# Layer norm, attention and a ternary feed-forward on one core: keys and queries by Strassen's seven products

## The chip, the cores and the metric

The kernel runs on one core of a Trainium2 chip. The core has a matrix engine (TensorE, PE in the profile; its weight loads are shown apart as PEld), a vector engine (VectorE, DVE), an engine for functions of one argument (ScalarE, ACT), a general engine (GpSimd, POOL) and an engine that mainly issues DMAs (SyncE, SP). ACT and POOL can issue DMAs too. Each engine works through its own queue in order; across engines they wait for each other by semaphores. Data sits in SBUF (128 partitions); TensorE writes to PSUM[...].

The metric is the device time of one execution in microseconds, as the median of several runs. A profiled execution, a run of its own, gives the trace.

## The reference

The input x has 2048 tokens of 256 values. With xn the layer norm of x, the result is x + attention(xn) + ffn(xn). Attention has 16 heads of 128 values; the feed-forward has ternary weights and a hidden width of 704.

```python
qkv = jnp.einsum('bsd,ed->bse', x, Wqkv)          # 3 x 16 heads x 128
q, k, v = ...
logits = jnp.einsum('bqhd,bkhd->bhqk', q, k) * D ** (-0.5)
w = softmax(logits)
out = jnp.einsum('bhqk,bkhd->bqhd', w, v).reshape(B, S, H * D)
return jnp.einsum('bse,de->bsd', out, Wout)
...
hidden = jax.nn.sigmoid(x1) * x2                   # x1, x2: xn by quantized w1, w2
return _bitlinear(hidden, w3)
```

Per head, q and k are each a product of a 128 x 256 weight with the 256 x 2048 transposed xn.

## The kernel before

All matmuls of the attention are in fp32. The transposed xn (`xnT`, 128 x 2 x 2048: the 256 features as two chunks of 128 partitions) stays in SBUF. The 2048 tokens are four blocks of 512 (`QB`), each of four tiles of 128 queries. The work of the attention is a list of 64 `blocks`, 16 heads by 4 token blocks, hence 256 tiles `v`.

The feed-forward is done first, up to about 103 us; it leaves its part of the result, with x added, in the four tiles `ys` in SBUF, one per token block. The attention's output adds to them head after head, and the last head's sums are stored from there.

One loop (L544) runs over the tiles. The order of every engine's queue is the order of the program's text (`tc.manual_schedule`). In an iteration tile `v` gets its scores, and tile `u = v - 6` (`LEAD`) is weighted; `n, t` are block and tile of `u`, and `h, b` head and token block of `v`. In a tile:

- `scores` (L421): four matmuls of 128 x 512, two into each of two PSUM tiles "s" of two banks (three such tiles exist); after each half VectorE takes the maximum (`mx`, L439), then the negated maximum of both (`nm`, L444), and ScalarE the two exps (L452), whose results are the halves `p`.
- `exchanged` (L458): 16 DMAs of 64 KB that move 32-partition groups of `p` into `part` (three buffers), the first ten issued by SP, the other six by ACT.
- `transposed` (L473): VectorE transposes 32 x 32 blocks of `part` of tile `v - 2` into `pT`, in two instructions of 1024 elements.
- `weighted` (L481): four of the block's sixteen matmuls with v into the bank "av"; the block's last is followed by a copy to `oT` by ScalarE.
- by `t`, one further piece of work, all through a single PSUM bank "m" (pool `ps_m`): t = 0 a piece of v for a later group of two heads (`v_piece`, L126), t = 1 the output of the block before, in two halves (`projected`, L505, with sums into `ys` at L521 by VectorE), t = 2 a piece of k of the next head (`k_piece`, L100, copied to `kT` by ScalarE, L110), t = 3 a piece of q (`q_piece`, L112, scaled and copied at L121).

Because `v - u` is 6, t = 2 and t = 3 are the first and second tile of a block in the counting of `v`. A piece of k or q is two matmuls of 128 x 512 that accumulate over the two feature chunks. Keys are stored in an order of columns that suits the exchange: k's matmul reads `xnT` in runs of 32 columns (`xnT_k`, L98).

The weights wq and wk of two heads (a group `G`) come in by one DMA each on SP (`load_weights`, L73), as do those of v and of the output.

Of the kernel before, what the change touches and what calls it, by code (L numbers as in the profile page):

```python
# [8 lines left out]
F32 = mybir.dt.float32  # L9
F32R = mybir.dt.float32r  # L10
AF = mybir.ActivationFunctionType
ALU = mybir.AluOpType
# [7 lines left out]
def layernorm_attention_bitffn_kernel(  # L20
# [14 lines left out]
    nc = tc.nc  # L35
    P = 128
    S, DM = x.shape
    FF = w1T.shape[1]
    D = P
    HD = woutT.shape[0]  # L40
    H = HD // D
    KC = DM // P
    QB = 512
    NB = S // QB
    TB = QB // P
    NKT = S // P
    KQ = NKT // TB
    HALF = S // 2
    FC = -(-FF // P)
    G = 2  # L50
# [13 lines left out]
    make_identity(nc, ident)  # L64


    ys = [const.tile([P, TB, DM], F32, tag=f"y{c}", name=f"y{c}") for c in range(NB)]
    xnT = const.tile([P, KC, S], F32, tag="xnT", name="xnT")

    weights = {}  # L70
    lead_in = True

    def load_weights(g: int, what: str):  # L73

        if what == "o":
            w = wpool.tile([P, G, DM], F32, tag="wo", name=f"wo{g}", bufs=2)
            src = woutT[g * G * D : (g + 1) * G * D, :].rearrange("(h p) e -> p h e", p=P)
        else:
            w = wpool.tile([P, KC, G * D], F32, tag=f"w{what}", name=f"w{what}{g}")
            lo = "qkv".index(what) * HD + g * G * D  # L80
            src = wqkvT[:, lo : lo + G * D].rearrange("(c p) e -> p c e", p=P)
        nc.sync.dma_start(w, src)
        weights[g, what] = w


# [26 lines left out]
    def q_piece(h: int, c: int):  # L112
        w = weights[h // G, "q"]
        pm = bank([P, QB], f"pq{h}_{c}")
        for d in range(KC):
            nc.tensor.matmul(  # L116
                pm, w[:, d, bass.ts(h % G, D)], xnT[:, d, bass.ts(c, QB)],
                start=(d == 0), stop=(d == KC - 1),
            )
        qT = kvpool.tile([P, QB], F32, tag="qT", name=f"qT{h}_{c}", bufs=NB + 1)  # L120
        nc.scalar.activation(qT, pm, AF.Copy, scale=SCALE)  # L121
        qTs[h, c] = qT

    NV = NKT // 2

# [15 lines left out]
    ppool = ctx.enter_context(tc.tile_pool(name="ppool", bufs=2))  # L141
    front = ExitStack()
    fw = front.enter_context(tc.tile_pool(name="ffw", bufs=1))


    def loads(fraw):
# [186 lines left out]
    def added(c: int):  # L333

        yT = yTs.pop(c)
        if c < NB - 1:
            pt = ps_s.tile([P, 2, QB], F32, tag="s", name=f"pyt{c}")
            pts = [pt.rearrange("p a (b e) -> p (a b) e", e=DM)]
        else:
            pts = [bank([P, 2, DM], f"pyt{c}_{u}") for u in range(2)]  # L340
        m = TB // len(pts)
        for u, pt in enumerate(pts):
            for t in range(m):
                for e in range(DM // P):
                    nc.tensor.transpose(  # L345
                        pt[:, t, bass.ts(e, P)], yT[:, e, bass.ts(u * m + t, P)], ident
                    )
            y = ys[c][:, u * m : (u + 1) * m]
            nc.vector.tensor_tensor(y, pt, y, ALU.add)


    with tc.manual_schedule():
# [63 lines left out]
    SP_DMAS = 10  # L416

    blocks = [(h, b) for h in range(H) for b in range(NB)]
    sums, rinvs, oTs, parts, pTs, avs = {}, {}, {}, {}, {}, {}

    def scores(v: int, amid=None, late=None):  # L421

        n, t = divmod(v, TB)
        h, b = blocks[n]
        halves, ps = [], []
        mx = small.tile([P, 2], F32, tag="mx", name=f"mx{v}")  # L430
        for i in range(2):
            s = ps_s.tile([P, HALF], F32, tag="s", name=f"s{v}_{i}")
            for j in range(HALF // QB):
                nc.tensor.matmul(  # L434
                    s[:, bass.ts(j, QB)], qTs[h, b][:, bass.ts(t, P)],
                    kTs[h][:, i * HALF + j * QB : i * HALF + (j + 1) * QB],
                    start=True, stop=True,
                )
            nc.vector.tensor_reduce(mx[:, i : i + 1], s, AX.X, ALU.max)  # L439
            halves.append(s)  # L440
            if i == 0 and amid:
                amid()
        nm = small.tile([P, 1], F32, tag="nm", name=f"nm{v}")
        nc.vector.tensor_reduce(nm, mx, AX.X, ALU.max, negate=True)  # L444
        if t == 0:
            sums[n] = small.tile([P, TB, 2], F32, tag="sum", name=f"sum{n}")
        if late:
            late()
        part = ppool.tile([P, NQ, S // NQ], F32, tag="part", name=f"part{v}", bufs=3)
        for i, s in enumerate(halves):  # L450
            p = ppool.tile([P, HALF], F32, tag="p", name=f"p{v}_{i}", bufs=4)
            nc.scalar.activation(  # L452
                p, s, AF.Exp, bias=nm, accum_out=sums[n][:, t, i : i + 1],
            )
            ps.append(p)
        parts[v] = ps, part

    def exchanged(v: int):  # L458
        ps, part = parts[v]
        for j in range(NQ):  # L460
            for g in range(NQ):
                (nc.scalar if NQ * j + g >= SP_DMAS else nc.sync).dma_start(
                    part[bass.ts(j, 32), g, :],
                    ps[j // 2][bass.ts(g, 32), bass.ts(j % 2, S // NQ)],
                )

    def inverses(n: int):
        ri = small.tile([P, TB], F32, tag="ri", name=f"ri{n}")
# [4 lines left out]
    def transposed(v: int):  # L473
        n, t = divmod(v, TB)
        if t == 0:
            pTs[n] = apool.tile([P, TB, NQ, S // NQ], F32, tag="pT", name=f"pT{n}")
        part = parts.pop(v)[1]
        for g in range(0, NQ, 2):
            nc.vector.transpose(pTs[n][:, t, g : g + 2], part[:, g : g + 2])  # L479

    def weighted(n: int, k: int, part=None):  # L481

# [22 lines left out]
    def projected(n: int, u: int, pool=ps_m, tag: str = "m"):  # L505

        h, b = blocks[n]

        m = 1 if n == NBK - 1 and u else 2
        pms = []  # L510
        for j in range(2):
            if j % m == 0:
                pm = pool.tile([P, m, DM], F32, tag=tag, name=f"po{n}_{u}_{j}")
            pms.append(pm[:, j % m, :])
            nc.tensor.matmul(  # L515
                pms[j], oTs[n, 2 * u + j], weights[h // G, "o"][:, h % G, :],
                start=True, stop=True,
            )
        for j in range(2):
            t = 2 * u + j  # L520
            nc.vector.scalar_tensor_tensor(  # L521
                ys[b][:, t, :], pms[j], rinvs[n][:, t : t + 1], ys[b][:, t, :],
                ALU.mult, ALU.add,
            )

            if h == H - 1 and (j or n == NBK - 1):
                t0 = t if n == NBK - 1 else t - 1
                (nc.scalar if n == NBK - 1 and j else nc.sync).dma_start(
                    out[b * QB + t0 * P : b * QB + (t + 1) * P, :].rearrange(
                        "(t p) d -> p t d", p=P  # L530
                    ),
                    ys[b][:, t0 : t + 1, :],
                )

    NBK = len(blocks)
    GB = G * NB
# [6 lines left out]
    with tc.manual_schedule():  # L543
        for u in range(-LEAD, (NBK - 1) * TB):  # L544
            n, t = divmod(u, TB)
            v = u + LEAD
            lead_in = u < 0
            if v < NBK * TB:

                scores(  # L550
                    v,
                    amid=(lambda: added(NB - 1)) if v == 1 else None,
                    late=(lambda: [summed(fp, c, f) for c, f in chunks[-2:]]) if v == 0 else None,
                )
                h, b = blocks[v // TB]

            if lead_in:
                for what, hg, i in first.get(v, ()):
                    {"q": q_piece, "k": k_piece, "v": v_piece}[what](hg, i)
                if v == 1:  # L560
                    front.close()
                    apool = ctx.enter_context(tc.tile_pool(name="apool", bufs=2))
                    load_weights(1, "v")
            elif t == 0:
                g = n // GB + 1
                if g < H // G and ("v", g, n % GB) not in made:
# [7 lines left out]
            elif t == 2:  # L574
                if n % GB == 1 and n // GB + 1 < H // G:
                    load_weights(n // GB + 1, "o")
            if v < NBK * TB and h + 1 < H:
                if v % TB == 0 and ("k", h + 1, b) not in made:
                    k_piece(h + 1, b)
                elif v % TB == 1 and ("q", h + 1, b) not in made:  # L580
                    q_piece(h + 1, b)
                if h % G == 0 and b == NB - 1 and h // G + 1 < H // G:
                    if v % TB == 2:
                        load_weights(h // G + 1, "k")
                    elif v % TB == 3:
                        load_weights(h // G + 1, "q")
            if v < NBK * TB and t != TB - 1:
                exchanged(v)
            if u >= 0:
                for k in range(t * KQ, (t + 1) * KQ):  # L590
                    weighted(n, k)
            if v < NBK * TB and t == TB - 1:
                exchanged(v)
            if u == (NBK - 1) * TB - 1:
                inverses(NBK - 2)
                inverses(NBK - 1)
            if v > 1 and v - 2 < NBK * TB:
                transposed(v - 2)
            if u >= 0 and t == 1 and n:
                projected(n - 1, 1)  # L600

        n = NBK - 1
        for k in range(NKT):
# [46 lines left out]
```

## Time and profile before

| what | value |
|---|---|
| median of 3 runs | 2285.8 us (2285.75 to 2285.82) |
| the profiled execution | 2285.53 us, its span 2283.7 us |
| VectorE: maxima of the scores, L439 | 512 instructions of 1224 ns mean |
| VectorE: transposes, L479 | 512 of 1222 ns |
| VectorE: sums into y, L521 | 256 of 478 ns |
| ScalarE: exp, L452 | 512 of 1109 ns |
| ScalarE: copies of k (L110), q (L121) | 64 of 582 ns, 64 of 594 ns |
| exchange, L462 | 2560 DMAs by SP, 1536 by ACT, 64 KB each, landing 2.0 us after issue |
| DMA engines | 284.90 MB in all, 125 GB/s mean |

A row of the profile gives line, engine and operation, the tiles written and read, the shape and the count, the busy time and the mean of one. An fp32 matmul of the source shows as two records in the trace. Matmul records overlap, because they are pipelined; their distance from start to start is what one costs. In a timeline the columns are start and duration in microseconds, engine, line, operation, output<-inputs, count, and in brackets the engine's idle time before and what ended it. The span is a little shorter than the time of the execution, which also has what lies around it.

### The profile page before, as it was taken

The numbers are of one execution on the slowest core, as the hardware profiler recorded it, in microseconds if no ns is written. First come the engines' busy times: TensorE is split into PE (matmuls) and PEld (weight loads), VectorE is DVE, ScalarE is ACT, GpSimd is POOL, SyncE is SP. The second block draws the span as 40 slices with busy tenths as digits, with TensorE's granted clock in tenths as the row PEclk, the third lists the DMA queues.
The fourth block names the chain that finished last, engine by engine and source line by source line (L and its number), as shares of the span: only waits on it lengthen the run. The fifth ranks groups of instructions, "written<-read, shape, count | busy, mean of one in ns | idle before, by whom it ended". The sixth has DMA issues, their size and how long they took to land.

```text
span 2283.7 us, 22775 instructions
## 1 busy us (share of the span) xinstructions
PE 2276.2 (100%) x6026; PEld 1138.0 (50%) x6026; DVE 1464.4 (64%) x1809; ACT 768.6 (34%) x1363; POOL 1.1 (0%) x8
## 2 busy tenths in 40 slices
PE   9999999999999999999999999999999999999999
PEld 6744444444444444444444444444444444444445
DVE  6667666566566566566666666666666666666675
ACT  5543333333333333333332332333333333333331
POOL 0000000000000000000000000000000000000000
PEclk9999999999999999999999999999999999999999
DMA  2065555555555545555555555555555455455555
GB/s 94 6 160 143 130 123 127 127 132 123 127 122 129 136 116 127 130 122 136 123 119 131 130 127 127 121 125 139 121 123 131 119 138 125 118 126 129 132 141 133
DMA packets 211090, 284.90 MB, mean 125 GB/s; under 512 B 66384, under 2 KB 79376, under 8 KB 210960
## 3 DMA queue, kind: packets, MB, share of 16 engines
q1 hardware_dynamic: 136256, 181.77, 32.8%
q10 hardware_dynamic: 74704, 101.68, 18.6%
q8 instruction: 47, 0.77, 0.2%
q14 instruction: 83, 0.68, 0.1%
HBM read 12.65 MB, written 2.10 MB: 6 GB/s over the span
## 4 chain that ended last, share of the span: by engine, by line
PE 99%; ACT 0%; DVE 0%; DMA 0%; issue 0%; DVEq 0%
PE s L434 38%; PE av L489 38%; PE pv L132 5%; PE po L515 5%; PE pq L116 5%; PE pk L106 5%; PE ph L300 2%; PE pf L323 1%; PE pyt L345 0%; DMA y<-in_x_dram 0%; ACT xnT L225 0%; PE pxn L221 0%; ACT v L137 0%; DVE y L521 0%; DVE st L193 0%
## 5 line engine op out<-in xcount | busy, mean ns | idle before, releaser
L439 DVE TENSOR_REDUCE mx<-s 128x1 f32<-128x1024 f32 x512 | 626.8, 1224 | 702.8 <-PE s L434 702.7
L452 ACT ACTIVATE p<-s,nm 128x1024 f32<-128x1024 f32 x512 | 565.5, 1109 | 1390.4 <-DVE nm L444 596.7
L434 PE MATMUL s<-kT,qT 128*128 128x512 f32 x2048 | 920.9, 592 | 0.0
L489 PE MATMUL av<-pT,v 128*128 128x512 f32 (+1 forms) x2080 | 920.4, 586 | 0.0
L479 DVE STREAM_TRANSPOSE pT<-part 128x1024 f32<-128x1024 f32 x512 | 606.3, 1222 | 22.7 <-DMA part<-p 11.4
L434 PEld LDWEIGHTS s<-kT,qT 128*128 128x128 f32 x2048 | 389.0, 190 | 461.9 <-issue 439.8
L489 PEld LDWEIGHTS av<-pT,v 128*128 128x128 f32 x2080 | 395.2, 190 | 434.7 <-issue 427.1
L515 PE MATMUL po<-wo,oT 128*128 128x256 f32 x512 | 131.5, 379 | 0.5 <-DVE oT L498 0.5
L515 PEld LDWEIGHTS po<-wo,oT 128*128 128x128 f32 x512 | 97.2, 190 | 66.9 <-issue 59.1
L521 DVE SCALAR_TENSOR_TENSOR y<-po,ri,y 128x256 f32<-128x256 f32 x256 | 111.8, 478 | 18.3 <-PE po L515 3.5
L132 PE MATMUL pv<-wv,xnT 128*128 128x256 f32 x512 | 121.0, 380 | 1.3 <-ACT xnT L225 1.3
L116 PE MATMUL pq<-xnT,wq 128*128 128x512 f32 x256 | 120.4, 592 | 0.7 <-ACT xnT L225 0.7
L106 PE MATMUL pk<-xnT,wk 128*128 128x512 f32 x256 | 120.0, 592 | 0.0
L132 PEld LDWEIGHTS pv<-wv,xnT 128*128 128x128 f32 x512 | 96.9, 190 | 39.2 <-issue 27.0
L452 ACT ACTIVATION_READ_ACCUMULATOR p<-s,nm 128x1 f32 x512 | 100.3, 196 | 0.0
L116 PEld LDWEIGHTS pq<-xnT,wq 128*128 128x128 f32 x256 | 48.6, 190 | 60.4 <-issue 59.3
L106 PEld LDWEIGHTS pk<-xnT,wk 128*128 128x128 f32 x256 | 48.6, 190 | 59.5 <-issue 58.8
L501 ACT COPY oT<-av 128x512 f32<-128x512 f32 x64 | 37.2, 581 | 61.1 <-PE av L489 61.1
L444 DVE TENSOR_REDUCE nm<-mx 128x1 f32<-128x2 f32 x256 | 39.7, 155 | 27.9 <-DVE mx L439 0.9
L121 ACT ACTIVATE qT<-pq 128x512 f32<-128x512 f32 x64 | 38.0, 594 | 3.8 <-PE pq L116 3.8
L137 ACT COPY v<-pv 128x512 f32<-128x512 f32 x64 | 37.1, 582 | 4.9 <-PE pv L132 4.8
L110 ACT COPY kT<-pk 128x512 f32<-128x512 f32 x64 | 37.1, 582 | 1.5 <-PE pk L106 1.5
(74 smaller groups left out, 318.4 us busy)
## 6 DMA issues: line engine op xcount, KB each, us to landing
part<-p SPq DMA_DIRECT2D x2560, 64.0 KB, 2.0
part<-p ACTq DMA_DIRECT2D x1536, 64.0 KB, 2.0
wv<-in_wqkvT_dram SPq DMA_DIRECT2D x8, 256.0 KB, 3.0
wq<-in_wqkvT_dram SPq DMA_DIRECT2D x8, 256.0 KB, 2.9
wk<-in_wqkvT_dram SPq DMA_DIRECT2D x8, 256.0 KB, 3.0
wo<-in_woutT_dram SPq DMA_DIRECT2D x8, 256.0 KB, 2.8
out_dram<-y SPq DMA_DIRECT2D x6, 256.0 KB, 2.4
y<-in_x_dram SPq DMA_DIRECT2D x2, 512.0 KB, 7.2
```

Of the source, the lines that this page charges most:

```text
L106: nc.tensor.matmul(pm, w[:, d, bass.ts(h % G, D)], xnT_k[:, d, c], start=(d == 0), stop=(d == KC - 1),)
L116: nc.tensor.matmul(pm, w[:, d, bass.ts(h % G, D)], xnT[:, d, bass.ts(c, QB)], start=(d == 0), stop=(d == KC - 1),)
L132: nc.tensor.matmul(pm[:, j, :], xnT[:, d, bass.ts(2 * i + j, P)], w[:, d, :], start=(d == 0), stop=(d == KC - 1),)
L300: nc.tensor.matmul(ph[:, j, :], w[:, d], xs[c][i][:, d], start=((d, i) == todo[0]), stop=((d, i) == todo[-1]),)
L434: nc.tensor.matmul(s[:, bass.ts(j, QB)], qTs[h, b][:, bass.ts(t, P)], kTs[h][:, i * HALF + j * QB : i * HALF + (j + 1) * QB], start=True, ...
L439: nc.vector.tensor_reduce(mx[:, i : i + 1], s, AX.X, ALU.max)
L444: nc.vector.tensor_reduce(nm, mx, AX.X, ALU.max, negate=True)
L452: nc.scalar.activation(p, s, AF.Exp, bias=nm, accum_out=sums[n][:, t, i : i + 1],)
L479: nc.vector.transpose(pTs[n][:, t, g : g + 2], part[:, g : g + 2])
L489: nc.tensor.matmul(av, vs[h // G, k // 2][:, k % 2, bass.ts(h % G, D)], pTs[n][:, t0:t1].rearrange("p t g (k q) -> p (t g) k q", q=32)[:, ...
L515: nc.tensor.matmul(pms[j], oTs[n, 2 * u + j], weights[h // G, "o"][:, h % G, :], start=True, stop=True,)
L521: nc.vector.scalar_tensor_tensor(ys[b][:, t, :], pms[j], rinvs[n][:, t : t + 1], ys[b][:, t, :], ALU.mult, ALU.add,)
```

## The change

For heads 2 to 15, keys and queries of two neighbouring token blocks are made together: the two outputs (k, q) by two blocks are a 2 x 2 arrangement of products over the two feature chunks, and Strassen's scheme (in Winograd's form) makes it with seven products of 128 x 512 in place of eight. Heads 0 and 1 are made as before.

- The sums of the inputs that the scheme needs are made by GpSimd: `x_sums` once, eight operations of 128 x 512; `weight_sums` per head, four of 128 x 128.
- The products (`fast_product`) are single matmuls into the bank "m", two in a tile for the first two tiles of an even block and the first tile of an odd one, one for the second tile of an odd block. Where a tile has two, the second comes after two or three of the four matmuls of `weighted` (`ahead`).
- VectorE, in place of ScalarE, reads the products (`fast_read`, `fast_scaled`): it adds them up in `kT` and `qT`, which serve as the running sums. The first read stands behind `nm`, the second behind the transposes.
- `ys` no longer stay in SBUF: they are stored to DRAM (`yds`) at the start, and each block's part is loaded by a DMA of GpSimd (`fetched`) before its output sums and stored again (`put_away`) after them.
- `part` is two half tiles of two buffers each; `exchanged` follows the transposes in the text, and its 16 DMAs go in another order.
- wq and wk are loaded by GpSimd's queue.

```diff
+    def weight_sums(h: int):
+        wk, wq = (weights[h // G, i][:, :, bass.ts(h % G, D)] for i in "kq")
+        w = wpool.tile([P, 4, D], F32, tag="ws", name=f"ws{h}")
+        add, sub = ALU.add, ALU.subtract
+        nc.gpsimd.tensor_tensor(w[:, 0], wq[:, 0], wq[:, 1], add)
+        nc.gpsimd.tensor_tensor(w[:, 1], w[:, 0], wk[:, 0], sub)
+        nc.gpsimd.tensor_tensor(w[:, 2], wk[:, 0], wq[:, 0], sub)
+        nc.gpsimd.tensor_tensor(w[:, 3], wk[:, 1], w[:, 1], sub)
...
+    def x_sums(c: int):
+        t = apool.tile([P, 4, QB], F32, tag=f"t{c}", name=f"t{c}", bufs=1)
...
+        for i, (a, b) in enumerate(((x01, x00), (x11, t[:, 0]), (x11, x01), (x10, t[:, 1]))):
+            nc.gpsimd.tensor_tensor(t[:, i], a, b, ALU.subtract)
...
+    def fast_product(h: int, b: int, i: int, second: bool):
...
+        lhs, rhs = {
+            (0, 0): ((wk[:, 0], x00), (w[:, 1], t[:, 1])),
+            (0, 1): ((w[:, 2], t[:, 2]), (wq[:, 1], t[:, 3])),
+            (1, 0): ((w[:, 0], t[:, 0]), (w[:, 3], x11)),
+            (1, 1): ((wk[:, 1], x10),),
+        }[b % 2, i][second]
+        pm = ps_m.tile([P, QB], F32, tag="m", name=f"pw{h}_{b}_{i}_{int(second)}")
+        nc.tensor.matmul(pm, lhs, rhs, start=True, stop=True)
...
+    def fast_read(h: int, b: int, i: int, second: bool, pm):
...
+        k0, k1 = (
+            kTs[h].rearrange("p (j k r) -> p k j r", j=P // 32, r=32)[:, j * TB : (j + 1) * TB]
+            for j in (c, c + 1)
+        )
...
+        def q_sum(q, base):
+            nc.vector.scalar_tensor_tensor(q, pm, SCALE, base, ALU.mult, ALU.add)
+
+        def k_sum(k, base):
+            nc.vector.tensor_tensor(k, pk, base, ALU.add)
+
+        if (b % 2, i) == (0, 0):
+            if not second:
+                nc.vector.tensor_copy(k0, pk)
+            else:
+                k_sum(k1, k0)
+        elif (b % 2, i) == (0, 1):
+            if not second:
+                q_sum(q1, q0)
+            else:
+                q_sum(q0, q1)
+        elif (b % 2, i) == (1, 0):
+            if not second:
+                q_sum(q1, q1)
+            k_sum(k1, k1)
+        else:
+            k_sum(k0, k0)
+
+    def fast_scaled(h: int, b: int):
...
+        nc.vector.tensor_scalar(q0, k1, SCALE, None, ALU.mult)
...
+        nc.sync.dma_start(yds[c], ys[c])
...
+        parts[v] = [
+            ppool.tile([P, 2, S // NQ], F32, tag=f"part{i}", name=f"part{v}_{i}") for i in range(2)
+        ]
+        todo = [(j + 2 * a, g + 2 * i) for a in range(2) for i in range(2) for j in range(2) for g in range(2)]
...
+            seven = 2 <= h + 1 < H and v % TB < 2
+            hi = h + 1, b, v % TB
...
+                if seven:
+                    pms.append(fast_product(*hi, False))
+                    fast_read(*hi, False, pms[0])
...
+            if b == NB - 1 and h + 2 < H:
+                if h % G == 0 and v % TB in (0, 2):
+                    load_weights(h // G + 1, "qk"[v % TB // 2], nc.gpsimd)
+                if v % TB == 3:
+                    weight_sums(h + 2)
+            first_of_pair = (b % 2, v % TB) == (0, 0)
+            twice = seven and (b % 2, v % TB) != (1, 1)
+            ahead = KQ // 2 if first_of_pair else KQ - 1
             if u >= 0:
-                for k in range(t * KQ, (t + 1) * KQ):
+                for k in range(t * KQ, t * KQ + ahead):
                     weighted(n, k)
-            if v < NBK * TB and t == TB - 1:
-                exchanged(v)
+            if twice:
+                pms.append(fast_product(*hi, True))
...
             if v > 1 and v - 2 < NBK * TB:
                 transposed(v - 2)
+            if twice:
+                fast_read(*hi, True, pms[1])
+            if seven and first_of_pair:
+                fast_scaled(h + 1, b)
+            if more and t != TB - 1:
+                exchanged(v)
+            if u >= 0:
+                for k in range(t * KQ + ahead, (t + 1) * KQ):
+                    weighted(n, k)
+            if more and t == TB - 1:
+                exchanged(v)
             if u >= 0 and t == 1 and n:
                 projected(n - 1, 1)
+            if t == 2 and n >= 0:
+                if n:
+                    put_away(n - 1)
+                fetched(n)
```

## The prediction

> **What bounds the kernel now.** I read the engines' totals first, then the chain of work that ended last, then the clock, and only then one tile in order of time.
>
> ```profile
> span 2283.7 us, 22775 instructions
> ...
> PE 2276.2 (100%) x6026; PEld 1138.0 (50%) x6026; DVE 1464.4 (64%) x1809; ACT 768.6 (34%) x1363; POOL 1.1 (0%) x8
> ...
> PEclk9999999999999999999999999999999999999999
> ...
> PE 99%; ACT 0%; DVE 0%; DMA 0%; issue 0%; DVEq 0%
> PE s L434 38%; PE av L489 38%; PE pv L132 5%; PE po L515 5%; PE pq L116 5%; PE pk L106 5%; PE ph L300 2%; PE pf L323 1%; PE pyt L345 0%; DMA y<-in_x_dram 0%; ACT xnT L225 0%; PE pxn L221 0%; ACT v L137 0%; DVE y L521 0%; DVE st L193 0%
> ```
>
> TensorE is busy all the time and makes up 99% of the chain, at an undiminished clock. No other engine has its work on the path; pq and pk, the products that the change touches, are on it with 5% each. A busy row alone could hide bubbles between matmuls, so the pitch decides. The timeline of one tile (t = 3 of the loop, where q of the next head is made):
>
> ```profile
> 1018.72 3.60 PE L434 MATMUL s<-kT,qT 128*128 128x512 f32 x8
> ...
> 1020.64 1.23 DVE L439 TENSOR_REDUCE mx<-s 128x1 f32<-128x1024 f32 x1 [2.96 <-PE s L434]
> ...
> 1022.15 1.88 PE L116 MATMUL pq<-xnT,wq 128*128 128x512 f32 x4
> ...
> 1022.35 1.23 DVE L439 TENSOR_REDUCE mx<-s 128x1 f32<-128x1024 f32 x1 [0.49 <-PE s L434]
> ...
> 1023.68 0.15 DVE L444 TENSOR_REDUCE nm<-mx 128x1 f32<-128x2 f32 x1
> 1023.87 3.60 PE L489 MATMUL av<-pT,v 128*128 128x512 f32 x8
> 1023.89 2.37 DVE L479 STREAM_TRANSPOSE pT<-part 128x1024 f32<-128x1024 f32 x2
> ...
> 1027.30 3.60 PE L434 MATMUL s<-kT,qT 128*128 128x512 f32 x8
> ```
>
> From s to s the tile takes 1027.30 - 1018.72 = 8.58 us and holds 8 + 4 + 8 = 20 records, so a record of 512 columns costs 0.429 us with no gap. A matmul of the source is two records (the program has 1024 for s, the trace 2048): 0.858 us each. The other thing to see is VectorE: it does mx, mx, nm and the transposes, then waits 2.96 us for the next scores. It has room, and follows TensorE.
>
> **What the Trainium skill says.** "Trainium Kernel Development and Optimization", Performance Expectations, warns that matmul busy time is a poor measure because matmuls are pipelined; the trace agrees (rows of 592 ns mean at a pitch of 429), so I count pitches. "VectorE: DVE Perf Modes", the walkthrough of Mode 1x, says that this mode takes fp32, strides and PSUM operands alike at one result per cycle. The trace agrees for PSUM and fp32: L349's sum takes 680 ns for 512 elements and 1216 for 1024, or 1.05 ns per element; rows in runs of 32 elements, as the change writes them, no run shows yet. "GPSIMD Engine Reference", Instruction dispatch, gives about 2.5 cycles per element for a Pool operation with two inputs; at its 1.2 GHz I estimate 1.07 us for 512 columns and 0.27 us for 128. "DMA: Bandwidth & Descriptors", Anatomy of one DMA (SWDGE), fits 2.0 us + bytes / 436e3: an estimate of 3.2 us for 512 KB; the trace's 512 KB loads at the start took 7.2 us, queued among others.
>
> **The change, part by part.**
>
> *Removed from TensorE.* Heads 2 to 15 are made from seven products for each pair of token blocks, two pairs a head. Before, 14 heads x 16 matmuls = 224; after, 14 x 14 = 196. So 28 matmuls go: 28 x 0.858 = 24.0 us. Everything else on TensorE keeps its count (s 1024, av 1040, v 256, output 256 matmuls). The saved matmul lies in one tile only: the second tile of an odd block has one product in place of two, 7.72 us in place of 8.58. Since TensorE is 99% of the chain, this is on the path in full unless TensorE starts to wait.
>
> *New waits on TensorE.* All products go through the one bank "m". Before, two matmuls accumulated into it and ScalarE emptied it after its two exps. Now a tile has two separate products, and the second must wait until VectorE has read the first. Take T0 as the end of s on TensorE (1022.15 above). VectorE starts the second mx at T0 + 0.20, nm at T0 + 1.53; the next instruction starts at T0 + 1.60 (where an operation without waits follows: ri at 1006.58 for T0 = 1004.98) to T0 + 1.74 (the transposes above). The reads' cost: a sum 0.685 (L307 and L349, same size); the scaled sum 0.745 (L521's 0.476 for 256 columns plus 256 x 1.05 ns); the copy between 0.58 (what ScalarE needs for the same, L110) and 0.69 (1x), I take 0.69; the scaling k1 to q0 from SBUF 0.49 (L257's slope of 0.52 ns per element from its 955 and 1022 ns) to 0.69. Then 0.05 us until TensorE's weight load (from oT L498, ending 2279.22, to L515's load at 2279.27), and the load of 0.19.
> - First tile of an even block: only two matmuls of av stand between the products, due T0 + 0.858 + 1.716 = T0 + 2.57. The read ends T0 + 2.29 to 2.43, so the matmul can start T0 + 2.53 to 2.67: a stall of 0 to 0.10. I take 0.05, 28 times = 1.4 us.
> - Second tile of an even block: three matmuls between, due T0 + 3.43; ready T0 + 2.59 to 2.73. No stall.
> - First tile of an odd block: two reads of one product (0.745 + 0.685, overlapping by 0.08 as L521's pairs do), ready T0 + 3.19 to 3.33; due 3.43. No stall, little to spare.
> - Second tile of an odd block: one product, no wait.
> Queued behind each waiting product are two (or one) av matmuls and the next s: a stall here is TensorE's own time, one for one.
>
> *VectorE's new work.* Per pair one copy, four sums, three scaled sums, one scaling: 0.69 + 2.74 + 2.24 + 0.49 = 6.2 us, 28 pairs = 172 us, some 1636 of 2262 us busy in all. It sits behind nm and behind the transposes, none of it ahead of nm. The fullest tiles end at about T0 + 6.2 (3.1 + 2.37 + 0.69), and the next mx is due at T0 + 7.06 (T0 + 6.2 after the short tile, which ends at T0 + 4.8). So it stays hidden; without that cover a microsecond here delays mx, nm, exp, and after 3.9 us of slack (exp of the first half ends T0 + 2.9, its bank is wanted T0 + 6.8) the scores. ScalarE loses 112 copies of 0.58 to 0.59 us, which were hidden: nothing.
>
> *The exchange.* "part" becomes two half tiles with two buffers each, in place of three whole ones, and the exchange is issued after the transposes: the 10 DMAs on SP and 6 on ACT now wait for the transposes of two tiles before. SP could start at exp's end, T0 + 2.9; now at the end of the first transpose, T0 + 2.8 without products and T0 + 3.5 to 4.3 with them. Ten issues at 0.6 us (590 ns median) end at T0 + 10.3 at the latest, land 2 us later, and are wanted by the transposes two tiles on (one of them short) + 1.6 = T0 + 17.9. ACT's six wait for the second transpose (T0 + 5.5 at worst) and end at T0 + 9.1; behind them stands the next exp, due T0 + 10.3. In the tile with the oT copy they end near T0 + 9.6, which can push the exp after a short tile by 0.1 us, inside the slack above. In head 15 (tiles of 6.87) SP already runs late in the trace of before: the last tile's first DMA is issued at 2259.31, its exps end at 2254.84. The new waits are met before SP is free there (the transposes of two tiles before end 2256.0). Cost 0, at most 4 us if SP's backlog grows beyond the 1.6 us that the last transposes (ending 2269.44) are ahead of their use at 2271.04.
>
> *y in DRAM.* Four stores on SP at the start, then 64 loads and 60 stores of 512 KB by Pool: 6.4 us of estimate per block of 34 us. The load of a block is issued in t = 2 and read in t = 1 of the next, three tiles or 25.7 us later: hidden; twice 7.2 us would be too. DMA engines are half busy (0.52 to 0.54 in whole heads), and get 65 MB on top of 285. The stores past the exchange of tile 0 on SP may hold the first transpose by some 2 us; TensorE has slack there. Cost 0, at most 1 us.
>
> *Pool.* Eight sums of x (8.6 us of estimate at tile 1, wanted from tile 16 on), 14 x 4 weight sums (1.1 us per head, in the last tile of a head and wanted by the second product of the next tile; ahead of them on Pool stand the load of wk, issued a tile earlier, and y's). The load of wq and wk leaves SP, 14 issues of 0.53, which were hidden. 0.
>
> Sum against the profiled execution: its time is 2285.53, with a span of 2283.7 and 1.8 us around it. 2285.53 - 24.0 + 1.4 = 2262.9. The median of the runs shown, 2285.8, lies 0.3 above it: **2263 us**.
>
> **Rivals.**
> 1. *The handover of bank "m" takes part of the gain.* If VectorE is later by d than the earliest times above, each pair loses (d - 0.04) in the first tile and (d - 0.24) in the odd one. For it: a spare of hundredths of a microsecond. Against it: mx starts 0.20 after its scores in both halves of the tile shown, so VectorE comes to the product on time. d = 0.4 gives 0.52 x 28 = 14.6 us: 2276; d = 0.25 gives 6 us: 2268.
> 2. *Slower: the reads in runs of 32 run at half speed.* Place: the copy and the sums into kT, between the two products of a tile. Price: 0.69 more in each, so d = 0.69: (0.65 + 0.45) x 28 = 30.8 us, and 2285.8 - 24.0 + 30.8 = 2293. It outweighs the gain from (d - 0.04) + (d - 0.24) = 0.858, d = 0.57, that is reads of 1.26 us. For it: no row of before shows VectorE on such rows. Against it: the skill's Mode 1x, and TensorE already reads xnT in such runs (L106) at 0.47 us per record (120.0 / 256), as L116 does without them (120.4 / 256).
> 3. *No change: another wait takes over.* If the short tile only makes the scores wait for exp or the transposes for the exchange, TensorE idles 0.86 in each: 2285. Against it: 3.9 us and 5 us of slack.
>
> **How the numbers follow.** Forecast 0.68 (2260 to 2267); rival 1 0.17 (2267 to 2281); rival 3 0.05; rival 2 0.10. A measurement of this kernel tells about 0.2%, 4.6 us, from no change. Faster 0.68 + 0.17 = 0.85, same 0.05, slower 0.10. The floor is the whole saving, 2261.8, and 1.8 us below it in case stalls that the modelled ends of matmuls hide go with the products: 2260. To leave out no more than 0.2 I reach into rival 1 by two thirds, to 2272.
>
> **What would show it.** Right: a TensorE still near 100%; 14 matmuls per head in place of 16; tiles of 8.58 but 7.72 for the second tile of an odd block; no wait of a product for VectorE above 0.1 us; the reads at 0.69 and 0.75; y's loads landing well before the output's sums ask. Wrong: idle time of TensorE ahead of a product (rival 1), reads above 1.2 us (rival 2), idle ahead of s or av (rival 3).

## The result, and the profile after

| kernel | median | range | runs |
|---|---|---|---|
| before | 2285.81 us | 2285.75 to 2285.82 | 4 |
| changed | 2266.57 us | 2265.73 to 2266.87 | 4 |

The changed kernel takes 0.9915 of the time before (95% interval 0.9898 to 0.9932): 19.2 us less, out of the 24.0 us that the removed matmuls are worth. The profiled execution took 2266.85 us, with a span of 2264.8. The page of it, from the same parts as shown of before, with the two rows of the sums and the loads of y:

```profile
span 2264.8 us, 24412 instructions
...
PE 2253.9 (100%) x5970; PEld 1126.4 (50%) x5970; DVE 1598.8 (71%) x2061; ACT 715.2 (32%) x1251; POOL 112.4 (5%) x210
...
PE 95%; DMA 2%; SPq 1%; DVE 1%; ACT 1%; ACTq 0%; issue 0%; DVEq 0%
PE s L530 37%; PE av L588 37%; PE pw L165 7%; PE pv L221 5%; PE po L614 5%; DMA part<-p 2%; PE ph L395 2%; PE pf L418 1%; SPq L562 1%; PE pq L115 0%; DVE pT L578 0%; ACTq L562 0%; PE pk L105 0%; ACT p L547 0%; DMA wv<-in_wqkvT_dram 0%
...
L188 DVE TENSOR_TENSOR kT<-pw,kT 128x512 f32<-128x512 f32 x112 | 74.6, 666 | 0.2 <-issue 0.2
...
L185 DVE SCALAR_TENSOR_TENSOR qT<-pw,qT 128x512 f32<-128x512 f32 x84 | 57.3, 683 | 0.2 <-issue 0.2
...
ya<-yd POOLq DMA_DIRECT2D x64, 512.0 KB, 4.2
```

The 56 records that are missing on PE (6026 to 5970) are the 28 matmuls, two records each. `pw` (7%) has taken the place of `pq` and `pk` (5% each). VectorE reads 512 columns of a product in 666 ns where it writes them into `kT` in runs of 32 columns, and in 683 ns for the scaled sums into `qT`, which have no such runs. The chain is the line to look at twice: TensorE's share fell from 99% to 95%, while its busy share stays at 100%. The chain walks back from the end to what released each step, and here it leaves TensorE at some places and goes through the exchange (`part<-p`, 2%, with SP's queue 1%). It can walk back a long way there; its 5% is not idle time. For that I took the distance from start to start of neighbouring matmul records of the attention and subtracted the pitch of 0.4295 us (half of it for 256 columns). What is left over:

| place (us from the span's start) | before | changed | what waits there |
|---|---|---|---|
| 119 to 142, the first tiles | 0 | 1.6 | scores (`s`) for the exps |
| 222, output of the second block | 0 | 1.0 | `po` for VectorE's sum |
| 2228 to 2252, the last blocks | 0 | 2.1 | scores for exp, then `av` for transposes |
| the end, output of the last block | 0.7 | 0.7 | `po` for `oT`, in every kernel here |
| all products of keys and queries | 0 | 0 | |

So 4.8 us more are lost than before, and none of it at a product. (The expectation of experiment 1 calls the place at 222 us the output of block 0. It is block 1, the second: the output matmuls of block 0 start at 185.75 and 190.05.) The timeline of two kinds of tile: first, part of the first tile of an even block, where VectorE's copy must come between two products, then a whole short tile, the second of an odd block (start and duration in us, engine, line, operation):

```profile
226.29 1.02 PE L165 MATMUL pw<-xnT,wk 128*128 128x512 f32 x2
...
227.15 1.88 PE L588 MATMUL av<-pT,v 128*128 128x512 f32 x4
...
227.90 0.68 DVE L192 COPY kT<-pw 128x512 f32<-128x512 f32 x1
...
228.87 1.02 PE L165 MATMUL pw<-t,ws 128*128 128x512 f32 x2
...
1012.13 3.60 PE L530 MATMUL s<-kT,qT 128*128 128x512 f32 x8
1015.56 1.02 PE L165 MATMUL pw<-xnT,wk 128*128 128x512 f32 x2
1016.42 3.60 PE L588 MATMUL av<-pT,v 128*128 128x512 f32 x8
1019.85 3.60 PE L530 MATMUL s<-kT,qT 128*128 128x512 f32 x8
```

The short tile takes 1019.85 - 1012.13 = 7.72 us. In the other, the second product starts at 228.87, 2.58 after the first: two matmuls of av and no gap. The copy had ended at 227.90 + 0.68 = 228.58.

Where the 4.8 us arise, the list of waits shows (engine, what it made, what it waited for; us in total, times, longest):

```profile
DVE pT L578 <- DMA part<-p: 37.0, 77, 5.0
...
PEld s L530 <- ACT p L547: 8.6, 18, 2.0
```

Transposes waited 37.0 us for the exchange, 77 times; before it was 11.4 us in 9 waits. Most of that cost nothing, the long ones did. The timeline around them, first GpSimd's queue near 203 us, then the last blocks:

```profile
203.41 0.72 POOL L81 DMA_DIRECT2D wq<-in_wqkvT_dram  x1 [70.10 <-PE pq L115]
204.12 0.57 POOL L649 DMA_DIRECT2D yd<-ya  x1
208.78 0.54 POOL L643 DMA_DIRECT2D ya<-yd  x1 [4.09 <-DMA yd<-ya]
209.31 0.72 POOL L81 DMA_DIRECT2D wk<-in_wqkvT_dram  x1
...
2219.62 7.25 ACTq L562 DMA_DIRECT2D part<-p  x6
2219.75 0.53 POOL L643 DMA_DIRECT2D ya<-yd  x1 [37.72 <-DVE pT L578]
...
2223.71 0.15 DVE L540 TENSOR_REDUCE nm<-mx 128x1 f32<-128x2 f32 x1
...
2225.61 1.88 PE L530 MATMUL s<-kT,qT 128*128 128x512 f32 x4
...
2227.37 1.11 ACT L547 ACTIVATE p<-s,nm 128x1024 f32<-128x1024 f32 x1 [7.41 <-DMA part<-p]
...
2228.62 2.37 DVE L578 STREAM_TRANSPOSE pT<-part 128x1024 f32<-128x1024 f32 x2 [4.75 <-DMA part<-p]
...
2228.62 1.98 PE L530 MATMUL s<-kT,qT 128*128 128x512 f32 x4 [1.13 <-ACT p L547]
...
2250.76 1.05 POOL L643 DMA_DIRECT2D ya<-yd  x2 [30.48 <-DVE pT L578]
```

At 203 us the load of wq had waited 70.1 us, because its buffer was still read by the q pieces of head 1. The first store of y, whose sums were done by 192 us, and the next load stood behind it in the same queue, and so 1.5 MB (two transfers of 512 KB and two of 256) go out within 7 us. The transposes of 215.46 then wait 3.97 us for the exchange; the tile's maxima come behind them, and the block's output sums behind these, at 220.96.

At 2219.75 it is one load of y alone that meets the exchange. How long it and the exchange's DMAs took from issue to landing, in the window from 2219 to 2227 us (size, median us):

```profile
ya<-yd POOLq DMA_DIRECT2D x1, 512.0 KB, 6.4
part<-p ACTq DMA_DIRECT2D x6, 64.0 KB, 5.3
```

ScalarE's six issues of the exchange span 7.25 us, but no single issue is slow: they take 0.51 to 0.71 us each, and the median of all in this trace is 0.59. What is slow is the landing: 5.3 us, where the exchange's DMAs land 2.0 us after issue when no large transfer is under way. On ScalarE's queue a DMA of the exchange goes out only when the fourth one before it has landed; this holds for all of them in the traces of both kernels. Here the fifth goes out at 2224.70, 0.02 after the first has landed, and the sixth 0.02 after the second. The exp behind them starts at 2227.37, although its nm was ready at 2223.86, and the scores wait for that exp. The four records of the scores from 2225.61 would have been followed by the next at 2225.61 + 4 x 0.43 = 2227.33; it comes at 2228.62. The transposes of 2228.62 have waited 4.75 us for the exchange too. Why this load takes 6.4 us, where the median of all 64 is 4.2, is not shown.

The loads of the last two blocks do go out one right after the other, but only at 2250.76, when the last DMA of the exchange has landed (2249.18). They slow none of it. The loss at 2252 is the end of a delay that was there before: the transposes that `av` waits for had started at 2249.26. That it is left over from 2228 is argued, not shown.

### The profile page after: what moved, and what is told of

It reads as the page before. It is cut to its first block, busy times and chain, and to the rows that moved or that the text cites. A ratio compares the mean times of both kernels' runs of the same rounds, so it can differ in the third digit from the quotient of the medians.

```text
span 2264.8 us, 24412 instructions
## 1 busy us (share of the span) xinstructions
PE 2253.9 (100%) x5970; PEld 1126.4 (50%) x5970; DVE 1598.8 (71%) x2061; ACT 715.2 (32%) x1251; POOL 112.4 (5%) x210
## 4 chain that ended last, share of the span: by engine, by line
PE 95%; DMA 2%; SPq 1%; DVE 1%; ACT 1%; ACTq 0%; issue 0%; DVEq 0%
PE s L530 37%; PE av L588 37%; PE pw L165 7%; PE pv L221 5%; PE po L614 5%; DMA part<-p 2%; PE ph L395 2%; PE pf L418 1%; SPq L562 1%; PE pq L115 0%; DVE pT L578 0%; ACTq L562 0%; PE pk L105 0%; ACT p L547 0%; DMA wv<-in_wqkvT_dram 0%
## 5 line engine op out<-in xcount | busy, mean ns | idle before, releaser
L588 PE MATMUL av<-pT,v 128*128 128x512 f32 (+1 forms) x2080 | 934.4, 586 | 0.3 <-DVE pT L578 0.3
L621 DVE SCALAR_TENSOR_TENSOR ya<-po,ri,ya 128x256 f32<-128x256 f32 x256 | 111.7, 478 | 18.1 <-issue 2.7
L649 POOL DMA_DIRECT2D yd<-ya x60 | 33.0, 550 | 1509.1 <-DVE ya L621 1481.7
L165 PE MATMUL pw<-t,ws 128*128 128x512 f32 x168 | 85.8, 592 | 0.0
L188 DVE TENSOR_TENSOR kT<-pw,kT 128x512 f32<-128x512 f32 x112 | 74.6, 666 | 0.2 <-issue 0.2
L185 DVE SCALAR_TENSOR_TENSOR qT<-pw,qT 128x512 f32<-128x512 f32 x84 | 57.3, 683 | 0.2 <-issue 0.2
L165 PE MATMUL pw<-xnT,wk 128*128 128x512 f32 x112 | 57.2, 592 | 0.0
L165 PEld LDWEIGHTS pw<-t,ws 128*128 128x128 f32 x168 | 31.7, 189 | 40.4 <-issue 33.7
L643 POOL DMA_DIRECT2D ya<-yd x64 | 34.0, 531 | 295.0 <-DMA yd<-ya 226.8
```

The lines of the kernel that those rows point to most:

```text
L165: nc.tensor.matmul(pm, lhs, rhs, start=True, stop=True)
L185: nc.vector.scalar_tensor_tensor(q, pm, SCALE, base, ALU.mult, ALU.add)
L188: nc.vector.tensor_tensor(k, pk, base, ALU.add)
L588: nc.tensor.matmul(av, vs[h // G, k // 2][:, k % 2, bass.ts(h % G, D)], pTs[n][:, t0:t1].rearrange("p t g (k q) -> p (t g) k q", q=32)[:, ...
L621: nc.vector.scalar_tensor_tensor(y[:, t, :], pms[j], rinvs[n][:, t : t + 1], y[:, t, :], ALU.mult, ALU.add,)
```

## The experiments

My theory (T1): the product saving arrives in full, and the 4.8 us that are missing are the price of y in DRAM. Its rivals: the new exchange (order, half tiles, after the transposes) costs it (T2), or, a third way, the reads of the products load VectorE so much that other things come late.

**1. Without y's transfers.** The changed kernel with one tile in SBUF (and a second for the last block) in place of the copies in DRAM; the four stores at the start and GpSimd's 124 transfers are gone.

```diff
-        nc.sync.dma_start(yds[c], ys[c])
...
+            nc.gpsimd.memset(y, 0.0)
+            only.append(y)
         else:
...
-        nc.gpsimd.dma_start(y, yds[blocks[n][1]])
+            y = only[0]
...
-        y = sofar.pop(n)
-        if blocks[n][0] < H - 1:
-            nc.gpsimd.dma_start(yds[blocks[n][1]], y)
+        sofar.pop(n)
```

> The changed kernel without the stores of y at the start and the 124 transfers of y by Pool: one tile in SBUF, cleared once, takes all output sums, so the input and the feed-forward are left out of the result and the four token blocks' sums run together. In the changed kernel's trace TensorE loses 4.8 us in three places (lead-in 1.6, the output of block 0 at 222 us 1.0, the last two blocks 2.1). Theory T1 (the bursts of y by Pool, 512 KB each, slow the exchange, the transposes wait, mx and exp come late): these go but for the 0.7 us of the kernel's end that the kernel before has too, 2262 to 2263 us. Rival T2 (the exchange in two half tiles with two buffers, issued after the transposes, is late by itself): 2266 to 2267, as the changed kernel.

Measured: 2261.96 us (2261.55 to 2262.07), ratio 0.9892 (0.9877 to 0.9907). From its page:

```profile
PE 2252.2 (100%) x5970; PEld 1126.8 (50%) x5970; DVE 1599.5 (71%) x2061; ACT 715.0 (32%) x1251; POOL 47.5 (2%) x88
...
PE 99%; ACT 0%; DMA 0%; DVE 0%; ACTq 0%; issue 0%; DVEq 0%
```

With VectorE's full new work (1599.5 us) and the new exchange in place, TensorE is 99% of the chain again. Against 2285.94, the median of before beside it, the saving is 23.98 us, where 28 x 0.858 is 24.0. Of the gaps, 0.35 us near 119 us are left besides the one at the end. T1 holds for the changed kernel, and nothing is left there for the other two to explain.

**2, 3 and 4. The parts put into the kernel before, alone and together.** First y in DRAM (the stores at the start, `fetched` and `put_away` at t = 2), then the new exchange, then both:

```diff
+        nc.sync.dma_start(yds[c], ys[c])
...
+            if t == 2 and n >= 0:
+                if n:
+                    put_away(n - 1)
+                fetched(n)
```

```diff
-        part = ppool.tile([P, NQ, S // NQ], F32, tag="part", name=f"part{v}", bufs=3)
...
+        parts[v] = [
+            ppool.tile([P, 2, S // NQ], F32, tag=f"part{i}", name=f"part{v}_{i}") for i in range(2)
+        ]
...
             if v > 1 and v - 2 < NBK * TB:
                 transposed(v - 2)
+            if v < NBK * TB and t != TB - 1:
+                exchanged(v)
```

> The kernel before with y stored to DRAM at the start and loaded and stored by Pool for each block as in the changed kernel; eight products, the exchange as it was. T1: slower by what the changed kernel lost, 2288 to 2291, with idle time of TensorE near the lead-in and in the last blocks. T2: 2285.5 to 2286.5, no difference.

> The kernel before with the exchange as in the changed kernel (two half tiles of two buffers each, issued after the transposes, the new order of the 16 DMAs); eight products, y in SBUF. T1: 2285.5 to 2286.5. T2: 2288 to 2291.

> The kernel before with y's traffic and the new exchange together (e2 and e3 in one), eight products. If the two costs only add, 2288 (2.1 + 0 over before). If the exchange's fewer buffers take away the room in which a burst of y is absorbed, more: 2289 to 2290.5, as e5, which has both and lies 4.1 over before.

| kernel before, with | median | range | ratio (interval) | beside it, before |
|---|---|---|---|---|
| y in DRAM | 2288.01 | 2287.15 to 2290.38 | 1.0007 (0.9999 to 1.0016) | 2285.94 |
| the new exchange | 2285.93 | 2285.43 to 2287.38 | 1.0000 (0.9992 to 1.0009) | 2285.94 |
| both | 2288.45 | 2287.6 to 2290.98 | 1.0008 (1.0000 to 1.0017) | 2286.04 |

The exchange alone costs nothing: T2 falls. The traffic of y costs 2.1 us there, less than half of the 4.6, with an interval that just reaches 1; with both it is 2.4, so the two hardly make each other worse.

**5. Eight products again.** The changed kernel with everything else kept: y in DRAM, the exchange, GpSimd's sums and loads.

```diff
-            seven = 2 <= h + 1 < H and v % TB < 2
+            seven = False
...
-            if h == 0:
+            if h + 1 < H:
...
-                if h % G == 0 and v % TB in (0, 2):
-                    load_weights(h // G + 1, "qk"[v % TB // 2], nc.gpsimd)
+                if h % G == 0 and v % TB in (2, 3):
+                    load_weights(h // G + 1, "kq"[v % TB - 2], nc.gpsimd)
```

> The changed kernel with the eight products back for heads 2 to 15 (pieces of k and q accumulated in the bank and copied by ScalarE); y's traffic, the exchange and Pool's sums stay, the loads of wk and wq stand in the last two tiles of a head as they did. If the scheme gives its whole saving of 28 matmuls and its reads by VectorE cost nothing, this is slower than the changed kernel by 24.0 us: 2290 to 2291. If the handover of the bank takes part of the saving, as forecast 1.4 us, 2289; if the losses come from the work that VectorE has with the products, 2286.

Measured: 2290.06 us (2287.93 to 2292.35), ratio 1.0018 (1.0011 to 1.0025). Against the changed kernel's 2266.57 that is 23.5 us: the scheme is worth that much also with its surroundings in place. The surroundings cost 4.1 us over before, about what the changed kernel misses, without one product read by VectorE: the third way falls too. Its gaps stand at the same places at the start and the end (140.75 us, 0.83; 2251 us, 1.19; 2275 us, 1.30). None stands near 222 us: here wk and wq are loaded in other tiles, and the first store of y goes out at 192.06 in place of 204.12. Experiment 4, with y and the exchange but without GpSimd's sums, explains only 2.4 of the 4.1. By the gaps, 0.9 us of the difference lies in the first tiles and 1.5 us in the last blocks. In the first tiles GpSimd's eight sums of x may be the reason: the first load of y goes out right after them, at 132.35, in experiment 4 at 124.22. In the last blocks the load at 2242.33 lands after 6.3 us, the same one in experiment 4 after 4.7. Neither cause is shown.

**6. One matmul of av between the products.** This asks how near the handover of bank "m" (the part of PSUM that holds one product of 128 x 512) is to costing something, and shows whether a late read would be seen at all.

```diff
-            ahead = KQ // 2 if first_of_pair else KQ - 1
+            ahead = 1 if first_of_pair else KQ - 1
```

> The changed kernel with one matmul of av in place of two between the two products of the first tile of an even block (the rest of the four follows after the second product). In the changed kernel's trace the copy of k ends 0.05 us before the second product's weight load would be late. If the handover is as worked out (release 0.05 us, load 0.19 us), each of the 28 pairs now stalls 0.858 - 0.05 = 0.81 us: 22.6 us in all, 2289 us. If there is hidden room (the load runs ahead of the wait), less: with 0.25 us of room 17 us, 2283.5.

Measured: 2289.48 us (2287.77 to 2292.75), ratio 1.0014 (1.0007 to 1.0021): 22.9 us over the changed kernel, 22.6 expected. The whole gain hangs on one matmul's place in the order. The timeline of such a tile:

```profile
434.67 1.02 PE L165 MATMUL pw<-xnT,wk 128*128 128x512 f32 x2
...
435.53 1.02 PE L588 MATMUL av<-pT,v 128*128 128x512 f32 x2
...
436.28 0.68 DVE L192 COPY kT<-pw 128x512 f32<-128x512 f32 x1
...
437.01 1.13 PE L165 MATMUL pw<-t,ws 128*128 128x512 f32 x2 [0.46 <-DVE kT L192]
```

The second product was due at 434.67 + 4 x 0.43 = 436.39 and starts at 437.01, which is 0.05 after the copy's end; its own two records stand 0.1 further apart than usual. Over the 28 such tiles the gaps add up to 21.6 us, 0.77 each.

**7. y's loads and stores spread out.** If three crowded places cause the loss, moving the transfers should give it back. The first load goes to SP's queue, wk of heads 2 and 3 is loaded earlier by SP, wq follows y's store in place of holding it up, and the last three blocks' loads go three blocks early, into the tiles of GpSimd's x sums and of the keys that are no longer read.

```diff
+        elif n > NBK - 4:
+            y = apool.tile([P, 4, QB], F32, tag=f"t{2 * (n - NBK + 3)}", name=f"ya{n}", bufs=1)
+            y = y[:, :2].rearrange("p a (t d) -> p (a t) d", d=DM)
...
-        nc.gpsimd.dma_start(y, yds[blocks[n][1]])
+        (nc.gpsimd if n else nc.sync).dma_start(y, yds[blocks[n][1]])
...
-                if h % G == 0 and v % TB in (0, 2):
+                if h and h % G == 0 and v % TB in (0, 2):
                     load_weights(h // G + 1, "qk"[v % TB // 2], nc.gpsimd)
+                if h == 0 and v % TB == 2:
+                    load_weights(1, "q", nc.gpsimd)
...
+            if v == TB + 2:
+                load_weights(1, "k", nc.sync)
...
-                fetched(n)
-                if n == NBK - 2:
-                    fetched(NBK - 1)
+                if n < NBK - 3:
+                    fetched(n)
+                if NBK - 7 < n < NBK - 3:
+                    fetched(n + 3)
```

> The changed kernel with y's transfers moved in time, the same number of them: the first load goes on SP's queue in its tile's turn and not at Pool's first chance; in head 0 wk is loaded by SP two blocks after the start and wq two tiles later, so that Pool's store and load of y do not stand behind them; the loads for the last three blocks come three blocks early, into the places of x's sums and of kT, which are free by then. Theory T1 (bursts that meet a busy exchange cost TensorE 1.0 us at 141 us, 1.0 at 222 us and some 2 in the last two blocks): 2262.5 to 2264. Rival (it is the mean load, not the bursts): 2265.5 to 2267, as the changed kernel.

Measured: 2264.52 us (2263.47 to 2265.05), ratio 0.9904 (0.9889 to 0.9918), 2.1 us under the changed kernel and a little above what was expected. The stalls near 141 and 222 us are gone, those after 2228 too, but 1.0 us is lost in a new place, at 2190 to 2192, after two loads at 2179.60 and 2180.12.

**8. Only the end of that.** The last three blocks' loads early, nothing else.

> The changed kernel with only the loads of y for the last three blocks moved three blocks forward. T1: the stalls at 141 and 222 us stay, those of the last two blocks go: 2264.5 to 2265.2. Rival (mean load): 2266 to 2267.

Measured: 2266.99 us (2266.12 to 2270.29), ratio 0.9918 (0.9903 to 0.9932): no gain, where 1.4 to 2.1 us were expected. The stalls after 2228 are gone, and others stand where the early loads now run, two in a row each time. One of them:

```profile
2123.76 1.05 POOL L646 DMA_DIRECT2D ya<-yd  x2 [3.79 <-DMA yd<-ya]
...
2125.59 7.57 ACTq L562 DMA_DIRECT2D part<-p  x6
...
2134.55 1.98 PE L530 MATMUL s<-kT,qT 128*128 128x512 f32 x4 [0.88 <-ACT p L547]
```

It is the picture of 2219 us again, here with two loads in a row: the exchange's DMAs land after up to 6.5 us, ScalarE's six issues span 7.57 us, its exp comes late, and the scores wait. In the changed kernel these three places (2123, 2152 and 2181 us) have one load each, the exchange's DMAs beside them land after 4.2 us at most, and nothing is lost. So this run made three pairs out of single loads.

**9. The stores doubled.** Is it the mean load of the DMA engines, or what happens at these few places? Every one of the 60 stores is done twice, into a second copy that nobody reads, 31 MB more.

```diff
             nc.gpsimd.dma_start(yds[blocks[n][1]], y)
+            nc.gpsimd.dma_start(yxs[blocks[n][1]], y)
```

> The changed kernel with each of Pool's 60 stores of y done twice, the second time to a place that nobody reads: 31 MB more. T1: more tiles in which the exchange comes late, and the loads behind the stores come 4 us later; 2268 to 2275. If the exchange has room between the three places, the stores cost nothing there: 2266 to 2267.5.

Measured: 2267.38 us (2267.03 to 2268.04), ratio 0.9917 (0.9902 to 0.9932): 0.8 us over the changed kernel, for 60 further transfers. The same stretch in the middle of the two kernels, changed and doubled (window and its length, busy time and count of PE, PEld, DVE, ACT, POOL, clock, DMA share, GB/s):

```profile
1100.00:1237.40 137.40, 137.40 (x355) 67.19 (x354) 98.40 (x126) 41.24 (x73) 6.04 (x12) 1.00 0.61 157
```

```profile
1100.00:1237.40 137.40, 137.40 (x356) 67.35 (x355) 98.07 (x124) 40.90 (x72) 8.27 (x16) 1.00 0.67 174
```

With 0.67 of the DMA engines in use TensorE is still busy for all of the 137.40 us. The gaps of the doubled kernel stand near 127, 142, 223, 2229 and 2252 us, much as in the changed one. The time lies under the 2268 to 2275 that T1 expected and in the range of the other case: more load on average costs little.

Nor is a slow landing enough to cost something. The doubled kernel's DMAs in the window from 265 to 273 us:

```profile
ya<-yd POOLq DMA_DIRECT2D x1, 512.0 KB, 7.0
part<-p ACTq DMA_DIRECT2D x6, 64.0 KB, 5.6
```

They are slower than those at 2219 us in the changed kernel, and no gap follows. What the places with losses have in common are tiles of only 6.87 us (131.47 to 138.34, 206.36 to 213.23 and 2218.75 to 2225.61 in the changed kernel); the doubled kernel's tile from 266.85 to 274.57 takes 7.72. That the shorter tiles leave too little time for the exchange is argued from this; no run changes the length of a tile alone.

**10. One at a time.** Experiment 7 with its last three loads given to ScalarE's queue, one per block at t = 0, two tiles away from GpSimd's own store and load. Queue, time and distance change together.

```diff
-        nc.gpsimd.dma_start(y, yds[blocks[n][1]])
+        queue = nc.sync if n == 0 else nc.scalar if n > NBK - 4 else nc.gpsimd
+        queue.dma_start(y, yds[blocks[n][1]])
...
-                fetched(n)
-                if n == NBK - 2:
-                    fetched(NBK - 1)
+                if n < NBK - 3:
+                    fetched(n)
+            if t == 0 and NBK - 6 < n < NBK - 2:
+                fetched(n + 2)
```

> As e6 in head 0, but the loads of y for the last three blocks go on ScalarE's queue, one at a time, each two tiles away from Pool's own, in place of two at once. T1 (single bursts that meet a late exchange): the stall of e6 at 2190 us (1.0 us) goes as well, 2262.8 to 2264. Rival (mean load): as e6, 2264.5, or worse, since ScalarE's queue now carries them: 2265 to 2266.

Measured: 2262.83 us (2262.11 to 2266.00), ratio 0.9902 (0.9885 to 0.9918). The timeline of the same place in the last blocks, where no load of y is under way now:

```profile
2218.10 3.74 ACTq L562 DMA_DIRECT2D part<-p  x6
...
2223.23 2.37 DVE L578 STREAM_TRANSPOSE pT<-part 128x1024 f32<-128x1024 f32 x2 [0.69 <-DMA part<-p]
...
2224.29 3.60 PE L530 MATMUL s<-kT,qT 128*128 128x512 f32 x8
```

ScalarE's six issues span 3.74 us in place of 7.25, the transposes wait 0.69 in place of 4.75, and the eight records of the scores follow each other. The gaps left are 0.5 us each near 119 and 127 us. This version is 3.7 us under the changed kernel by the medians; the two intervals against before overlap, one of its four runs was at 2266.0, and it is the gaps of the traces (1.8 us in place of 5.5) that carry the statement. It beats both kernels with all of y's bytes still moved.

## Why the prediction was right, and where it was not

The mechanism of the saving was as predicted, and the time lies in the range. Two terms of the sum were off, and that the time still lies in the range is in part luck: its upper end, 2267, is 0.4 us away, and with the stall of 1.4 us that was also forecast the kernel would have passed it.

- *Removed from TensorE, 24.0 us on the path in full:* right. Experiment 1 measured 23.98, and the tiles are 7.72 us.
- *The stall at bank "m", 1.4 us:* measured 0. The reads came at the early end of the estimate (the copy ended 2.29 us after the scores' end), and the step after them was priced too high: I put 0.05 + 0.19 between the read and the product, while in experiment 6 the product starts 0.05 after the copy and loses another 0.1 between its two records. So the changed kernel has 228.87 - 0.05 - 228.58 = 0.24 us to spare there, and one matmul less in between costs the whole gain.
- *VectorE's 172 us, hidden:* right. It is busy 1599 us, 134 more than before and not 172: the rows of the new work add up to 163 us (sums at 666 in place of 685 ns, scaled sums at 683 in place of 745, the scaling at 427 in place of 490), and they overlap their neighbours in time, which my sum left out. Experiment 1 has all of it and no stall from it.
- *The exchange, cost 0:* right by itself (experiment 3, -0.01 us). The loss in head 15, for which I kept up to 4 us, was 2.1 us and came through y's loads.
- *y in DRAM, "Cost 0, at most 1 us":* this is the mis-sized term; it measured 2266.57 - 2261.96 = 4.6 us. I asked whether the loads land before they are read. They do, but for the last pair: VectorE's sums wait for it until 2254.31, without a loss to TensorE. I did not ask what they do to others while they run. The part on the exchange counts on landings of 2 us and leaves 1.2 us between ScalarE's six issues (T0 + 9.1) and the next exp (T0 + 10.3) in a full tile; at 2219 us the landings took 5.3 us, and this room was gone. One of the places could be read from the code beforehand: the store and load of y stand in GpSimd's queue behind a load of wq that waits for head 1. I had named the queue's order for the weight sums only. The call of `fetched(NBK - 1)` right behind `fetched(NBK - 2)` looks like another, but that pair came after the exchange.
- *GpSimd, 0:* no cost of its operations is shown. They took longer than estimated (below).

-24.0 + 4.6 = -19.4 accounts for the measured -19.2. The two errors have opposite signs: 4.6 - 1.4 = 3.2 of the 3.6 us by which the median lies above the forecast. Of the rivals, the first (handover) and the second (half speed) did not happen: no gap at a product, reads under 0.7 us. The third's sign was there, idle time ahead of s and av, but not its mechanism: none of it lies in the tiles that the change shortened.

## What to carry to other kernels

A background transfer has two prices: whether it lands in time, and what it slows down while it runs. For the second, look less at the mean load than at the places where the work has little time to spare, here the shorter tiles at the start and in the last head, and at transfers that pile up there, for example behind a wait in a shared queue. And where a read is put between two uses of one bank, measure the spare time and what the next place in the order would cost: here 0.24 us to spare, and 22.9 us one place earlier.

## What the runs showed of the hardware that was not expected

- 31 MB more, spread over the kernel, cost 0.8 us; y's transfers in the changed kernel, 65 MB, cost 4.6 us, and 3.7 of it went when some loads and stores were moved, with all bytes kept.
- One load of 512 KB slows the landing of the small DMAs beside it, not their issue: in the changed kernel the exchange's DMAs landed after 2.0 us (median) with no large transfer under way and 3.0 us beside one load of y, up to 6.2 at 2219 us, with issues of 0.59 us (median) in both cases. Since the fifth of ScalarE's six waits for the landing of the first, the six then span 7.25 us, against 3.74 in the same place without a load.
- The Trainium skill, "DMA: Bandwidth & Descriptors", Anatomy of one DMA (SWDGE), gave an estimate of 3.2 us for 512 KB; GpSimd's loads of that size landed after 4.2 us (median), beside the exchange.
- The Trainium skill, "GPSIMD Engine Reference", Instruction dispatch: the estimates of 1.07 and 0.27 us met 1.27 us for 512 columns and 0.46 for 128. The slope, (1274 - 454) / 384 = 2.1 ns per element, is what the page says (2.5 cycles at 1.2 GHz); by these two sizes a fixed part of about 0.18 us per instruction comes on top, an estimate.
